# A gated, byte-quantized product and a signed layer on one Trainium2 core: bytes turned as 4-byte words, kv's bytes left in the low bytes of float16, and a list order chosen from 80 runs

## The chip, the cores and the metric

The kernel runs on one core of one Trainium2 chip. A core has a matrix engine (TensorE, "PE" in the profile; its weight loads are "PEld"), a vector engine (VectorE, "DVE"), a scalar engine (ScalarE, "ACT"), a general engine (GpSimd, "POOL") and a queue engine that issues the DMAs (SyncE, "SP"). Each works through its own list of instructions in order and waits on semaphores for the others. The metric is the time of one execution on the device in microseconds (us), smaller is better.

## The reference

`x` is float32 of 2 x 1024 x 2048, the context `kv` 2 x 2048 x 2048. What is computed, cut to the core:

```python
def fake_quant(x, scale, zp):
    q = jnp.clip(jnp.round(x / s + z), 0.0, 255.0)
    return (q - z) * s

def xattn(x1, x2):                       # scales and zero points are inputs, here 8/255 and 128
    return jnp.matmul(fake_quant(x1, ...), fake_quant(x2, ...))

def ffn(x, kernel, scale):               # kernel: 0/1, 2048 x 2048
    x_ei = jnp.concatenate([x[..., :1638], -4.0 * x[..., 1638:]], axis=-1)
    return scale * (x_ei @ kernel)

x = x + jnp.tanh(g_xattn[0]) * xattn(layernorm(x), ctx_4096)
x = x + jnp.tanh(g_ffn[0])   * ffn(layernorm(x), L0_ffn_kernel)
```

## The kernel before, in words

Rows of `x` come in 16 tiles of 128 rows: tiles 0 to 7 are the first batch, 8 to 15 the second. All large buffers are 4 KB-per-partition pages of one pool (44 of them).

**Product 1** (the quantized one). For each tile, VectorE takes the row statistics (`stats`, L362), small instructions make the row's factors, and `quant1` (L406 on ScalarE, L408 on VectorE) writes bytes `qn`. `shift1` (L414, ScalarE) subtracts 128, which makes bf16 or f16 values `q1`, and its accumulator gives the row sum `rsum`. The values are turned so that the contracted dimension lies on the partitions: tiles 0 to 3 by TensorE (`turn1`, L431, 16 transposes a tile into PSUM buffers `tr`, and `take1`, L423/L425, which copies them out), tiles 4 to 15 by a DMA transpose (`turn1_dma`, L441). `kv` is loaded in pieces of 128 x 1024 (`load_kv`, L445), quantized to bytes (`quant_kv`, L459 on ScalarE, L461 on VectorE) and shifted to bf16 or f16 (`shift_kv`, L468/L470) into pages `q2`. The matmuls of the first batch are `mm1` (L482): four column blocks of 512 by four pairs of tiles. Zero points other than 128 are put right with row sums (`tokb1`) and column sums: `sums_mm` (L494) lets TensorE add up a block's 16 slices with a matrix of ones, `sums_pair` (L503, L506) lets VectorE add them to two and leaves TensorE the last two (`sums_last`, L512). The results are added to `x` by `out1` (L524/L526), `add_row1` (L530) and `add_out1` (L534, GpSimd). In the second batch columns 0 and 1 go through one level of Strassen's scheme: seven products M1 to M7 per pair of tiles (`mm1s`, L584, `take1s` L596, `out1s` L603) over sums of halves made by VectorE (`right_sum` L547, `left_sum` L566/L568). Columns 2 and 3 are plain again.

**Product 2** (the layer with the 0/1 matrix). The normalized rows (`scale2` L623) are turned by TensorE as float32 (`turn2`, L630, `take2`), split into a high and a low float32r part (`part_hi` L676 on ScalarE, `part_lo` L680 on GpSimd or VectorE) and multiplied, again in Strassen's seven products, by slices of the matrix that ScalarE widens from bytes (`widen`, L720). The matmuls are `mm2` (L739): 1792 of 512 columns, the larger part of TensorE's work. `add2` (L754, VectorE) adds an accumulator to `back`, and `store2` stores it.

**The order.** Nothing above is issued as it is written. Each step is entered in a `Plan` with the engines that can do it and their costs (in units of some 0.22 us), the buffers that it reads, writes and opens, and, for the matmuls, a place in line. `Plan.dues` works out a due time for each step from the places of the matmuls that need it. `Plan.order` then walks once through time, gives each idle engine the ready step with the earliest due, and the resulting list is issued; that fixes every engine's instruction order. A step may begin once its due is nearer than `lead`; `port` marks VectorE steps that take turns with GpSimd in the plan. The pools' own semaphores keep the data right whatever the order.

```python
bytes_ = ctx.enter_context(tc.tile_pool(name="bytes", bufs=3))
BY_DMA = range(4, T)                      # tiles turned by a DMA
plan = Plan(dict(page=PAGES, acc=3, tr=2, q=3, qn=2, row=4, e=3, pair=2))
BY_PE = (True, True, True, False)         # blocks of the first batch summed by TensorE
order = plan.order({...}, {"SP": 13.0, "DVE": 22.0, "ACT": 22.0})
```

Of the kernel before, what the change touches and what calls it, by code (L numbers as in the profile page):

```python
# [19 lines left out]
P = 128  # L20
NB = 512
HB = 1024
EPS = 1e-5
CENTER = 128.0
# [3 lines left out]
class Op:  # L28
    __slots__ = ("engines", "f", "args", "deps", "users", "due", "lead", "opens", "uses",
                 "place", "end", "left", "index", "engine", "bias", "port")  # L30


class Plan:
# [21 lines left out]
    def op(self, engines, f, *args, reads=(), writes=(), opens=(), main=False, due=None, lead=80, bias=0.0,  # L55
# [7 lines left out]
        o.place = None  # L63
# [47 lines left out]
    def order(self, lag, start):  # L111


        self.dues()
        ready = {}
# [28 lines left out]
        while len(began) < len(self.ops):  # L144
            if not events:
                for e in engines:
                    if ready[e]:
                        print("stuck", e, [(o.f.__name__, o.args, o.due) for _, _, o in sorted(ready[e])[:4]])
                print(self.free, progress)
                raise RuntimeError("the plan is stuck")  # L150
# [5 lines left out]
            elif what == "idle":  # L156
                busy[o] = False
            else:
                for buf in o.uses:
                    if buf in self.count:  # L160
                        self.count[buf] -= 1
                        if not self.count[buf]:
                            self.free[self.kind[buf]] += 1
                for u in o.users:
                    u.left -= 1
                    u.end = max(u.end, now)
                    if not u.left:
                        for e in u.engines:
                            wait = 0.0 if e == o.engine and e != "SP" else lag.get((o.engine, e), lag[e])
                            push(now + wait, "ready", (e, u))  # L170
# [3 lines left out]
            while again:  # L174
                again = False
                for e in engines:
# [4 lines left out]
                    while ready[e]:  # L181
# [12 lines left out]
                        spare = 2 if o.due > progress + 40 else 0  # L194
# [24 lines left out]
        return [o for _, _, o in began]  # L219
# [3 lines left out]
def gated_xattn_ffn_kernel(  # L223
# [65 lines left out]
    kvv = kv.rearrange("b (k p) n -> b p k n", p=P)  # L289
# [17 lines left out]
    nc.vector.tensor_scalar(c2, z2, -1.0, CENTER, ALU.mult, ALU.add)  # L307
    f1 = const.tile([P, 1], F32, name="f1")
    nc.vector.tensor_scalar(f1, gate[:, 0:1], sc[:, 2:3], sc[:, 4:5], ALU.mult, ALU.mult)
    f1c1 = const.tile([P, 1], F32, name="f1c1")  # L310
# [4 lines left out]
    nc.vector.tensor_scalar(kc12, f1c1, c2, float(K), ALU.mult, ALU.mult)  # L315
# [5 lines left out]
    ident_bf = const.tile([P, P], BF, name="ident_bf")  # L321
    nc.vector.tensor_copy(ident_bf, ident)
# [6 lines left out]
    ones = const.tile([P, P], BF, name="ones")  # L329
    nc.gpsimd.memset(ones, 1.0)  # L330
# [3 lines left out]
    BY_DMA = range(4, T)  # L334
# [6 lines left out]
    DMA = 7.0  # L341
    ROOT = 8.0

    plan = Plan(dict(page=PAGES, acc=3, tr=2, q=3, qn=2, row=4, e=3, pair=2))
# [55 lines left out]
    def quant1(t: int, h: int, engine=None):  # L400

        if t not in qb:
            qb[t] = bytes_.tile([P, D], U8, tag="qn", name=f"qn_{t}", bufs=2)
# [6 lines left out]
    def shift1(t: int):  # L410

        q1[t] = page([D], F16 if t >= TPB else BF, f"q1_{t}")
        rsum[t] = small.tile([P, 1], F32, tag="rsum", name=f"rsum_{t}", bufs=8)
        nc.scalar.activation(q1[t], qb[t], AF.Copy, bias=-CENTER, accum_out=rsum[t])  # L414

    def tokb1(t: int):

        tokb[t] = small.tile([P, 1], F32, tag="tokb", name=f"tokb_{t}", bufs=T)
        nc.vector.tensor_scalar(tokb[t], rsum[t], f1c2, kc12, ALU.mult, ALU.add)
# [7 lines left out]
    def turn1(t: int, h: int):  # L427

        tr[t, h] = ps_tr.tile([P, KH, P], BF, tag="tr", name=f"tr1_{t}_{h}")
        for j in range(KH):  # L430
            nc.tensor.transpose(tr[t, h][:, j, :], q1[t][:, ts(h * KH + j, P)], ident_bf)  # L431

    def take1(t: int, h: int, engine=None):
        if h == 0:
            q1T[t] = page([KT, P], BF, f"q1T_{t}")
        copy(engine, q1T[t][:, ts(h, KH), :], tr.pop((t, h)))

    def turn1_dma(t: int):

        q1T[t] = page([KT, P], F16 if t >= TPB else BF, f"q1T_{t}")  # L440
        nc.sync.dma_start_transpose(out=q1T[t], in_=q1[t])  # L441

    def load_kv(b: int, c: int, g: int):
        stage[b, c, g] = page([2, NB], F32, f"kv_{b}_{c}_{g}")
        nc.sync.dma_start(stage[b, c, g], kvv[b, :, 2 * g : 2 * g + 2, ts(c, NB)])  # L445

    KEPT = ()

    def quant_kv(b: int, c: int, g: int, engine=None):

        if (b, c) in KEPT:
            if g % 4 == 0:
                qb[b, c] = page([4, HB], U8, f"q_{b}_{c}_{g // 4}")
            qb[b, c, g] = qb[b, c][:, g % 4, :]
        else:
            qb[b, c, g] = bytes_.tile([P, HB], U8, tag="q", name=f"q_{b}_{c}_{g}")
        v = flat(stage[b, c, g])
        if engine == "ACT":
            nc.scalar.activation(qb[b, c, g], v, AF.Identity, bias=z2, scale=rs2)  # L459
        else:  # L460
            nc.vector.tensor_scalar(qb[b, c, g], v, rs2, z2, ALU.mult, ALU.add)  # L461

    def shift_kv(b: int, c: int, g: int, engine=None):
        if g % 2 == 0:
            q2[b, c, g // 2] = page([4, NB], F16 if b else BF, f"q2_{b}_{c}_{g // 2}")
        half = flat(q2[b, c, g // 2][:, 2 * (g % 2) : 2 * (g % 2) + 2, :])
        if engine == "ACT":
            nc.scalar.activation(half, qb[b, c, g], AF.Copy, bias=-CENTER)  # L468
        else:
            nc.vector.tensor_scalar(half, qb[b, c, g], -CENTER, None, ALU.add)  # L470

# [18 lines left out]
    def sums_mm(b: int, c: int, ks):  # L490
        if ks[0] == 0:
            colsum[b, c] = ps_tr.tile([P, NB], F32, tag="tr", name=f"cs_{b}_{c}")
        for k in ks:
            nc.tensor.matmul(  # L494
                colsum[b, c], ones, rhs1(b, c, k), start=(k == 0), stop=(k == KT - 1)
# [18 lines left out]
    def row1(b: int, c: int):  # L514
        colrow[b, c] = rows.tile([P, NB], F32, tag="row", name=f"row_{b}_{c}")
        nc.scalar.activation(colrow[b, c], colsum.pop((b, c)), AF.Copy, scale=f1c1)

    def out1(b: int, c: int, tiles, i: int, engine=None):
# [4 lines left out]
        if engine == "ACT":  # L523
            nc.scalar.activation(ev[t, c], a, AF.Identity, bias=tokb[t], scale=f1)  # L524
        else:
            nc.vector.tensor_scalar(ev[t, c], a, f1, tokb[t], ALU.mult, ALU.add)  # L526
# [66 lines left out]
    def take1s(h: int, m: str, p: int):  # L593
        i, j = TAKES[m]
        xc = xt["x", 2 * p + i, h][:, ts(j, NB)]
        nc.vector.scalar_tensor_tensor(xc, acc1[SUM[m], h, p // 2][:, p % 2, :], f1, xc, ALU.mult, ALU.add)  # L596

    def out1s(h: int, m: str, p: int):
# [5 lines left out]
            ev[t, 2 * h + j], acc1[SUM[m], h, p // 2][:, p % 2, :], AF.Identity, bias=tokb[t], scale=f1  # L604
# [128 lines left out]

    def mm2(q: int, m: str, p: int, k: int, js=(0, 1)):
        if m in OPENS and k == 0:
            acc2[SUM[m], p] = ps_acc.tile([P, 2, NB], F32, tag="acc", name=f"acc2_{m}_{p}")
        for part in (hi, lo):
            for j in js:
                nc.tensor.matmul(  # L739
                    acc2[SUM[m], p][:, j, :],  # L740
# [11 lines left out]
    def add2(m: str, p: int, js=(0, 1)):  # L752
        v = back[(p,) + TAKES[m]][:, js[0] * NB : (js[-1] + 1) * NB]
        nc.vector.scalar_tensor_tensor(  # L754
            v, flat(acc2[SUM[m], p][:, js[0] : js[-1] + 1, :]), f2, v, ALU.mult, ALU.add
        )
# [15 lines left out]
    def ops_norm1(t: int, n: int, which: str, **when):  # L772
# [11 lines left out]
        for u in range(t, t + n):  # L784
            for h in range(2):
                op({"DVE": DVE(HB), "ACT": ACT(HB) + 0.9}, quant1, u, h, reads=[*both((which, u, h)), (("ra", u), 0)], writes=[(("qn", u), h)],
                   opens=[("qn", ("qn", u))] if h == 0 else [], port=True, **when)
            op({"ACT": ACT(D) + 0.9}, shift1, u, reads=both(("qn", u)), **when,
               writes=[(("q1", u), 0), (("rsum", u), 0)], opens=[("page", ("q1", u))])
            op({"DVE": 1.2}, tokb1, u, reads=[(("rsum", u), 0)], writes=[(("tokb", u), 0)], **when)  # L790
            if u in BY_DMA:
                op({"SP": 15.0}, turn1_dma, u, reads=[(("q1", u), 0)], writes=both(("q1T", u)),
                   opens=[("page", ("q1T", u))], **when)
                continue
            for h in range(2):
                op({"PE": 2.1}, turn1, u, h, reads=[(("q1", u), 0)], writes=[(("tr1", u, h), 0)],
                   opens=[("tr", ("tr1", u, h))], **when)
                op({"DVE": 3.2, "ACT": 4.6}, take1, u, h, reads=[(("tr1", u, h), 0)], writes=[(("q1T", u), h)],
                   opens=[("page", ("q1T", u))] if h == 0 else [], **when)

    def ops_kv(b: int, c: int, lead: float, by_pe: bool, lead2=None):

        lead2 = lead2 or lead
        for g in range(KG):
            v = (b, c, g)
            op({"SP": DMA}, load_kv, *v, writes=[(("kv",) + v, 0)], opens=[("page", ("kv",) + v)], lead=lead + 25)
            k = (("qb", b, c, g // 4), g % 4) if (b, c) in KEPT else (("qb",) + v, 0)
            op({"DVE": DVE(HB), "ACT": ACT(HB) + 0.9}, quant_kv, *v, reads=[(("kv",) + v, 0)], writes=[k],
               opens=[("page", k[0])] if (b, c) in KEPT and g % 4 == 0 else [] if (b, c) in KEPT else [("q", k[0])],
               lead=lead, port=True)  # L810
            w = ("q2", b, c, g // 2)
            op({"ACT": ACT(HB), "DVE": 3.3}, shift_kv, *v, reads=[k], writes=[(w, g % 2)],
               opens=[("page", w)] if g % 2 == 0 else [], lead=lead2, port=True)
# [68 lines left out]
    def ops_left_sums(p: int):  # L882
        for n, out, in0, in1 in ((3, "S3", "A11", "A21"), (1, "S1", "A21", "A22"), (2, "S2", "S1", "A11"),
                                 (4, "S4", "A12", "S2")):
            opens = [("page", ("q1S", p))] if n == 2 else []
            if n == 3:
                opens = [("page", ("q1S3", p))]
            op({"DVE": 3.3}, left_sum, p, n, reads=[half_key(p, in0), half_key(p, in1)],
               writes=[half_key(p, out)], opens=opens, lead=350.0, port=True)
# [10 lines left out]
    def ops_quad1(h: int, q: int):  # L900
# [11 lines left out]
        for m in ORDER1:  # L912
            acc = ("acc1", SUM[m], h, q)
            for p in pairs:
                for s in range(2):
                    op({"PE": 4.0}, mm1s, h, m, p, s, main=True, writes=[(acc, p % 2)],
                       reads=[half_key(p, LEFT1[m]), *both(right_key(m, h, s))],
                       opens=[("acc", acc)] if m in OPENS and p == pairs[0] and s == 0 else [],
                       in_turn=m in OPENS and p == pairs[0] and s == 0)
                i, j = TAKES[m]  # L920
                t = 2 * p + i
                v = ("x", t, h)
                if m in WITH_TOKENS:
                    e = ("e", t, 2 * h + j)
                    op({"ACT": 3.6}, out1s, h, m, p, reads=[(acc, p % 2), (("tokb", t), 0)], writes=[(e, 0)],
                       opens=[("e", e)], due=plan.place)
                    op({"POOL": GPS(NB)}, add_out1, 2 * h + j, t, reads=[(e, 0)], writes=[(v, j)], due=plan.place + 8)
                else:
                    op({"DVE": 3.6}, take1s, h, m, p, reads=[(acc, p % 2)], writes=[(v, j)], due=plan.place)
# [57 lines left out]
    def ops_product2(q: int, between):  # L987
        pairs = (2 * q, 2 * q + 1)
        for n, m in enumerate(ORDER):
# [25 lines left out]
            if q == T // 4 - 1 and n == len(ORDER) - 1:  # L1015
                steps[-LAG:] = tail
            for i, k, *js in steps:
# [3 lines left out]
                op({"PE": 2.1 * len(js)}, mm2, q, m, p, k, js, main=True, writes=[(acc, j) for j in js],  # L1021
                   reads=[(("hi", m, p), 0), (("lo", m, p), 0), (("wf", q, m, k), 0)],
                   opens=[("acc", acc)] if m in OPENS and k == 0 else [])
                if k == KH - 1:
                    v = ("back", p) + TAKES[m]
# [132 lines left out]
```

## Time and profile before

| | |
|---|---|
| median of 3 runs | 709.87 us (709.76 to 710.63) |
| the profiled execution, its own time | 710.47 us |
| its span, first to last instruction | 708.7 us |
| TensorE's clock | 1.000 of full, throughout |
| TensorE's first instruction, and its last record's end | 17.79 us, 704.46 us |
| ScalarE, VectorE, GpSimd busy | 482.6, 482.1, 306.5 us |
| DMA: moved, share of 16 engines | 162.07 MB, 68% |
| DMA packets under 512 B, of all | 29856 of 88396 |

How to read it: "busy" is the union of an engine's instruction records. Matmul records overlap (one lasts 0.38 us where one starts every 0.22 us), so TensorE's work is counted by the distance from one to the next. The span is what the instructions cover; the time of an execution is 1.8 us more in this one.

The last instructions, from the timeline (start us, length us, engine, line and operation, count, and in brackets the idle time before with what ended it):

```profile
702.00 0.75 DVE L754 SCALAR_TENSOR_TENSOR back<-acc_M,f,back 128x512 f32<-128x512 f32 x1 [1.89 <-PE acc_M L739]
...
702.81 0.50 PE L739 MATMUL acc_M<-wf_M,hi_M 128*128 128x512 f32 x1 [0.84 <-DVE back L754]
...
704.50 0.75 DVE L754 SCALAR_TENSOR_TENSOR back<-acc_M,f,back 128x512 f32<-128x512 f32 x1 [1.75 <-PE acc_M L739]
```

### The profile page before, as it was taken

The page shows a single profiled execution, that of the slowest core. Times are in us where ns is not written, and L with a number is a line of the kernel's source. Part 1 is how long each engine was busy: PE and PEld are TensorE (multiplying, and loading weights), DVE is VectorE, ACT ScalarE, POOL GpSimd, SP SyncE. Part 2 cuts the span into 40 slices and gives each one's busy share as a digit, 9 for nine tenths or more (in the row PEclk, how much of TensorE's full clock was granted, in tenths as well). Part 3 has the DMA queues.
Part 4 walks back from the last instruction along what each step waited for, and adds up shares of the span by engine and source line. Part 5 has one row for each costly group of instructions (what it writes and reads, how often), then busy time and mean ns, then how long its engine had stood idle before and what let it go on. Part 6 is the DMA issues. An engine that isn't in the chain of part 4 may idle for free.

```text
span 708.7 us, 8860 instructions
## 1 busy us (share of the span) xinstructions
PE 673.0 (95%) x3162; PEld 468.9 (66%) x3162; DVE 482.1 (68%) x725; ACT 482.6 (68%) x561; POOL 306.5 (43%) x186
## 2 busy tenths in 40 slices
PE   0699999999999999999999999999999999999997
PEld 0344444457778888878885444447888888888885
DVE  6989875799998778989978774458453335453331
ACT  4899853157689969989878832118689446679640
POOL 0048489983752403423337597874343001144000
PEclk9999999999999999999999999999999999999999
DMA  8999615959899999968589854338165279256032
GB/s 309 393 387 293 220 61 172 302 189 346 286 375 317 244 279 375 353 222 278 150 264 373 283 178 171 124 120 279 49 227 189 75 235 301 102 165 221 27 122 90
DMA packets 88396, 162.07 MB, mean 229 GB/s; under 512 B 29856, under 2 KB 46240, under 8 KB 88352
## 3 DMA queue, kind: packets, MB, share of 16 engines
q1 hardware_dynamic: 88352, 161.50, 68.4%
q8 instruction: 25, 0.41, 0.2%
q14 instruction: 19, 0.16, 0.1%
HBM read 117.44 MB, written 37.75 MB: 219 GB/s over the span
## 4 chain that ended last, share of the span: by engine, by line
PE 83%; DVE 6%; ACT 4%; POOL 3%; issue 2%; DMA 1%; SPq 0%; ACTq 0%; DVEq 0%; POOLq 0%
PE acc_M L739 53%; PE acc L482 19%; PE acc_M L584 6%; PE tr L630 3%; POOL x L534 2%; PE cs L494 2%; POOL x L530 2%; ACT wf_M L720 1%; DVE wB L705 1%; DMA x<-in_x_dram 1%; DVE bn_a L362 1%; DVE back L754 1%; DVE q L470 1%; ACT q L459 1%; ACT q L468 1%
## 5 line engine op out<-in xcount | busy, mean ns | idle before, releaser
L739 PE MATMUL acc_M<-wf_M,hi_M 128*128 128x512 f32 x896 | 282.2, 395 | 4.0 <-ACT wf_M L720 3.1
L739 PE MATMUL acc_M<-wf_M,lo_M 128*128 128x512 f32 x896 | 277.9, 391 | 0.5 <-POOL lo_M L680 0.5
L720 ACT ACTIVATE wf_M<-wr_M 128x1024 fp32r<-128x1024 uint8 x224 | 220.9, 1050 | 29.6 <-DMA wr_M<-in_wmask_dram 20.4
L739 PEld LDWEIGHTS acc_M<-wf_M,lo_M 128*128 128x128 f32 x896 | 168.1, 188 | 36.9 <-POOL lo_M L680 1.3
L739 PEld LDWEIGHTS acc_M<-wf_M,hi_M 128*128 128x128 f32 x896 | 163.9, 188 | 38.0 <-ACT wf_M L720 5.9
L482 PE MATMUL acc<-q,q1T 128*128 128x512 bf16 (+1 forms) x768 | 172.5, 382 | 0.5 <-DVE e L526 0.5
L680 POOL TENSOR_TENSOR lo_M<-A,hi_M 128x1024 fp32r<-128x1024 f32 x28 | 72.0, 2576 | 176.8 <-ACT hi_M L676 112.4
L754 DVE SCALAR_TENSOR_TENSOR back<-acc_M,f,back 128x1024 f32<-128x1024 f32 (+1 forms) x57 | 72.0, 1262 | 111.3 <-PE acc_M L739 96.3
L482 PEld LDWEIGHTS <-q1T 128*128 128x128 bf16 (+1 forms) x768 | 75.4, 98 | 90.5 <-issue 2.8
L530 POOL TENSOR_TENSOR x<-x,row 128x512 f32<-128x512 f32 x64 | 88.1, 1404 | 60.2 <-DMA kv<-in_kv_dram 38.0
L534 POOL TENSOR_TENSOR x<-x,e 128x512 f32<-128x512 f32 x64 | 91.9, 1454 | 42.7 <-ACT e L524 22.4
L524 ACT ACTIVATE e<-acc,tokb,f 128x512 f32<-128x512 f32 x30 | 22.7, 774 | 55.2 <-PE acc L482 50.7
L676 ACT CAST hi_M<-A 128x1024 fp32r<-128x1024 f32 x48 | 50.0, 1044 | 11.6 <-POOL A L664 7.9
L459 ACT ACTIVATE q<-kv,sc,rs 128x1024 uint8<-128x1024 f32 x41 | 49.8, 1232 | 5.3 <-DMA kv<-in_kv_dram 4.3
L362 DVE BATCH_NORM_STATS2 bn_b<-x 128x6 f32<-128x512 f32 x64 | 43.1, 686 | 14.9 <-POOL x L534 14.6
L423 ACT COPY A<-tr 128x512 f32<-128x512 f32 x33 | 19.2, 582 | 34.6 <-PE tr L630 34.6
L468 ACT ACTIVATE q<-q 128x1024 f16<-128x1024 uint8 (+1 forms) x39 | 40.3, 1046 | 0.4 <-DVE q L461 0.4
L526 DVE TENSOR_SCALAR e<-acc,f,tokb 128x512 f32<-128x512 f32 x18 | 14.5, 808 | 31.0 <-ACT e L524 26.9
L506 DVE TENSOR_TENSOR pair<-pair,q 128x1024 f16<-128x1024 f16 x30 | 30.8, 1033 | 2.9 <-ACT q L468 1.6
L414 ACT ACTIVATE q<-qn 128x2048 bf16<-128x2048 uint8 (+1 forms) x16 | 30.4, 1899 | 0.1
L680 DVE TENSOR_TENSOR lo_M<-A,hi_M 128x1024 fp32r<-128x1024 f32 x20 | 24.1, 1230 | 6.1 <-ACT hi_M L676 6.1
L461 DVE TENSOR_SCALAR q<-kv,rs,sc 128x1024 uint8<-128x1024 f32 x23 | 26.7, 1166 | 0.3
(99 smaller groups left out, 599.4 us busy)
## 6 DMA issues: line engine op xcount, KB each, us to landing
kv<-in_kv_dram SPq DMA_DIRECT2D x64, 512.0 KB, 9.9
x<-in_x_dram SPq DMA_DIRECT2D x32, 512.0 KB, 6.9
x<-x SPq DMA_DIRECT2D x32, 512.0 KB, 3.0
back<-x SPq DMA_DIRECT2D x32, 512.0 KB, 5.1
wr_M<-wt_T SPq DMA_DIRECT2D x32, 512.0 KB, 5.9
out_dram<-back SPq DMA_DIRECT2D x31, 512.0 KB, 4.1
wr_M<-in_wmask_dram SPq DMA_DIRECT2D x24, 512.0 KB, 5.9
n<-in_x_dram SPq DMA_DIRECT2D x16, 512.0 KB, 7.4
```

Of the source, the lines that this page charges most:

```text
L362: nc.vector.bn_stats(bn[v, t][:, c, :], xt[src[v, t, c // 2]][:, ts(c % 2, NB)])
L459: nc.scalar.activation(qb[b, c, g], v, AF.Identity, bias=z2, scale=rs2)
L468: nc.scalar.activation(half, qb[b, c, g], AF.Copy, bias=-CENTER)
L482: nc.tensor.matmul(acc1[b, c, tiles[0]][:, i, :], q1T[tiles[i]][:, k, :], rhs1(b, c, k), start=(k == 0), stop=(k == KT - 1),)
L530: nc.gpsimd.tensor_add(xc, xc, colrow[b, c])
L534: nc.gpsimd.tensor_add(xc, xc, ev.pop((t, c)))
L584: nc.tensor.matmul(acc1[key][:, i, :], left_half(p, LEFT1[m])[:, 4 * s + k, :], right1(m, h, s)[:, k, :], start=(m in OPENS and s == 0 and ...
L676: nc.scalar.copy(hi[m, p], A[left(m, p)])
L680: engines[engine].tensor_sub(lo[m, p], A[left(m, p)], hi[m, p].bitcast(F32))
L720: nc.scalar.activation(wf[q, m, k], wr[q, m, k // 4][:, k % 4, :], AF.Copy, bias=-float(RIGHT[m][1]))
L739: nc.tensor.matmul(acc2[SUM[m], p][:, j, :], part[m, p][:, k, :], wf[q, m, k][:, ts(j, NB)], start=(m in OPENS and k == 0 and part is hi), ...
L754: nc.vector.scalar_tensor_tensor(v, flat(acc2[SUM[m], p][:, js[0] : js[-1] + 1, :]), f2, v, ALU.mult, ALU.add)
```

## The change

1. **q1 is turned as bytes.** `shift1` and the DMA transposes go. `turn1` reads the 2048 bytes of a row as 512 float32 words: 4 transposes a tile, for all 16 tiles. `take1` reads the bytes of a word out of PSUM in steps of 4, subtracts 128 and writes f16. So slice 4w + j of the contracted dimension holds bytes j, j + 4, ...; `kv`'s rows are loaded in the same order ("(w p j)").
2. **Row sums** come from the bytes (`rowsum1`, ScalarE with its accumulator or VectorE's `tensor_reduce`), for tiles 0 and 1 from TensorE (`rowsum1_pe`, 16 matmuls of one column).
3. **kv's bytes stay bytes.** GpSimd fills a page with zeros (`fill_kv`), and `quant_kv` writes each byte into the low byte of a float16, which then is the byte times 2^-24. `shift_kv` goes. The factor 2^24 is put into the small constants (`f1u`, `f1c1u`), the zero point's 128 into others (`c2`, `kc12`, `kc12d`).
4. **Sums and orders.** Block 2 of the first batch goes from TensorE's sums to VectorE's pairs; the units of blocks and pairs run in another order; leads of the second batch change.
5. **Takes of the Strassen stage** are entered behind the matmuls of both pairs, and depend on the whole accumulator.
6. **The last pair's accumulator** for M5 and M3 is two single tiles of the pool `tr` instead of one of two halves.
7. **The list run** is repeated 80 times: each run shifts the due times of some steps, those that held up a matmul above all and others at random, and the list with the earliest planned end is issued.

```diff
-    def order(self, lag, start):
+    def order(self, lag, start, runs, seed=1):
...
+        for i in range(runs):
+            self.free, self.count = dict(free), dict(count)
+            try:
+                end = self.run(lag, start)
+            except RuntimeError:
+                end = None
+            if end is not None and (best is None or end <= best[0]):
+                best = end, self.began, [o.engine for _, _, o in self.began]
+                dues = [o.due for o in self.ops]
+                held = self.held_up()
+            for o, due in zip(self.ops, dues):
+                o.due = due
+            for ops in held:
+                if chance.random() < 0.5:
+                    step = chance.choice((3.0, 6.0, 12.0, 24.0))
+                    for o in ops:
+                        o.due -= step
...
-    kvv = kv.rearrange("b (k p) n -> b p k n", p=P)
+    kvv = kv.rearrange("b (w p j) n -> b p w j n", p=P, j=4)
...
+    def rowsum1_pe(t: int):
+        rsum[t] = ps_tr.tile([P, 1], F32, tag="tr", name=f"rs_{t}")
+        for k in range(KT):
+            nc.tensor.matmul(rsum[t], q1T[t][:, k, :], ones_h[:, 0:1], start=(k == 0), stop=(k == KT - 1))
...
-        for j in range(KH):
-            nc.tensor.transpose(tr[t, h][:, j, :], q1[t][:, ts(h * KH + j, P)], ident_bf)
+        for w in range(4):
+            nc.tensor.transpose(tr[t][:, w, :], qb[t].bitcast(F32)[:, ts(w, P)], ident)
...
+        v = flat(tr[t][:, 2 * h : 2 * h + 2, :]).bitcast(U8).rearrange("p (w t j) -> p w j t", w=2, j=4)
+        dst = q1T[t][:, ts(h, KH), :].rearrange("p (w j) t -> p w j t", j=4)
+        if engine == "ACT":
+            nc.scalar.activation(dst, v, AF.Copy, bias=-CENTER)
+        else:
+            nc.vector.tensor_scalar(dst, v, -CENTER, None, ALU.add)
...
+    def fill_kv(b: int, c: int, s: int):
+        q2[b, c, s] = page([4, NB], F16, f"q2_{b}_{c}_{s}")
+        nc.gpsimd.memset(flat(q2[b, c, s]).bitcast(F32), 0.0)
...
+        low = half.bitcast(U8).rearrange("p (n b) -> p n b", b=2)[:, :, 0]
...
+            nc.scalar.activation(low, v, AF.Identity, bias=z2, scale=rs2)
...
-    BY_PE = (True, True, True, False)
+    BY_PE = (True, True, False, False)
```

What this does to the lists of the engines, counted in the built programs: TensorE's transposes of q1 go from 64 of bf16 to 64 of float32 (4 a tile instead of 16, in 16 tiles instead of 4), sum matmuls from 48 and 10 to 32 and 12, and 32 one-column matmuls are new; L482 (768), L584 (224), L630 (256) and L739 (1792) keep their counts. ScalarE loses 39 shifts of kv and 16 of q1, and gets 22 half-tile takes instead of 4 and 7 row sums. VectorE loses 25 shifts, and gets 10 half-tile takes instead of 4, 7 row sums and 6 more halves of `part_lo`. GpSimd gets 32 fills and 6 halves of `part_lo` fewer.

## The prediction, made before the run

> **What bounds the kernel now.** The first view is the page: TensorE (PE) is busy 95% of the span, no other engine over 68%, and its idle slices are the first two and the last.
>
> ```profile
> span 708.7 us, 8860 instructions
> PE 673.0 (95%) x3162; PEld 468.9 (66%) x3162; DVE 482.1 (68%) x725; ACT 482.6 (68%) x561; POOL 306.5 (43%) x186
> ...
> PE   0699999999999999999999999999999999999997
> ```
>
> So two things can move the time: how early PE's steady stream starts, and how much issue time PE needs. The chain of waits, in order of time (start us, length, what), gives the start and the pitch of the matmuls:
>
> ```profile
> 1.19 5.44 DMA x<-in_x_dram
> ...
> 14.57 1.14 ACT qn L406
> 15.76 1.79 issue
> ...
> 20.85 1.22 ACT q L459
> 22.08 1.89 ACT q L414 x2
> 24.16 0.95 ACT q L468
> 25.21 1.01 PE cs L494 x2
> ...
> 170.73 0.44 PE tr L630 x4
> ...
> 447.23 31.94 PE acc L482 x148
> ...
> 516.99 70.88 PE acc_M L739 x312
> ```
>
> The chain runs load, statistics, quantize, ScalarE's pass from bytes to bf16 (L414, L468), and PE has work only from 25 us. The last two lines give pitches: a bf16 or f16 matmul 31.94/148 = 0.2158 us, a product-2 matmul 70.88/312 = 0.2272 us; L630 gives 0.11 us per float32 transpose. Durations of single records (272 ns for that transpose) overlap and are not added. Busy time by stretch (PE is the second figure) and PE's own waits:
>
> ```profile
> 0.00:17.70 17.70, 0.00 (x0) 0.00 (x0) 11.82 (x42) 8.64 (x11) 1.21 (x10) 1.00 0.88 309
> 17.70:45.00 27.30, 20.73 (x127) 11.02 (x128) 25.28 (x56) 24.49 (x28) 5.11 (x4) 1.00 1.04 390
> ...
> PE tr L431 <- ACT q L414: 17.8, 1, 17.8
> PE cs L494 <- ACT q L468: 5.5, 1, 5.5
> PE acc_M L739 <- ACT wf_M L720: 3.1, 3, 1.4
> PE acc_M L584 <- ACT e L603: 2.4, 3, 0.9
> PE acc_M L739 <- DVE back L754: 0.8, 1, 0.8
> ```
>
> By 45 us PE has issued 63 useful 512-column matmuls (127 less 64 transposes: 43 of L482, 20 of L494) and from there it is saturated. Check: after 45 us remain 1792 of L739 x 0.2272 = 407.1, 725 of L482 x 0.2158 = 156.5, 224 of L584 = 48.3, 256 transposes L630 x 0.11 = 28.2, 38 sum matmuls (28 of L494, 10 of L512) = 8.2: 648.3 us. From 45 us to PE's last record at 704.46 there are 659.5. PE thus loses 11.2 us after 45 us, of which the windows show 7.2 as idle; 4.2 us more follow PE (last add and store).
>
> **The change, part by part.**
>
> *Start.* Removed: the passes L414 (1.90 us a tile, plus 0.19 for the accumulator) and L468/L470 (1.05 or 0.69 us a half page) between quantizing and PE; now PE turns q1's bytes as float32 words, and kv is quantized straight into place. Loads land at 6.65 us and then one each 0.524 MB / 390 GB/s = 1.34 us. By the changed order (four x, nine kv, four x, kv again) load n lands at 6.65 + 1.34(n - 1): the eighth page of kv block 0 (n = 12) at 21.4, that of block 1 (n = 24) at 37.5. ScalarE quantizes tile 0 until 15.7 as before, PE turns it in 0.44, then two quantizations (2 x 1.23) stand before its two takes (1.1 each): the first matmul of the product at about 19.5 instead of 26. Tile 1's takes end near 23.5. Block 0 of the first pair, its sums and PE's row sums run until about 32, block 1 waits for its loads and ends at 37.5 + 0.8 (quantize) + 1.7 (eight matmuls) = 40.0. By then 64 of L482 and 32 sum matmuls are done: 96 against 63 at 45. The row sums (32 matmuls of one column, between 0.1 us, the weight load's row, and 0.22 each, so 3 to 7 us) lie in that wait for loads. If the loads came 2 us later, so would all.
>
> *Work on PE after that.* Product 2, L584 and L630 stay: 407.1 + 48.3 + 28.2. Of L482, 768 - 64 = 704 remain: 151.9. Sums: block 2 goes to VectorE pairs, so 12 matmuls: 2.6. New: 12 tiles turned by PE, 4 transposes each, 48 x 0.11 = 5.3 (the DMA transposes of 12 tiles go; 4 of the 16 tiles fall into the start). Total 643.4. [...]
>
> *Lost time.* Of the 11.2 us two parts should go: the last pair's accumulator becomes two tiles, so the 0.84 us for which PE waits on VectorE at 702 us goes; and product 1's takes move behind both pairs' matmuls, where PE is at the next accumulator, so up to 2.4 us on L603 go. New waits can come: each turned tile needs its bytes and one of two `tr` buffers in PE's order; behind a late one every matmul queues. Twelve such places at 0 to 0.4 us (the wait of L431 on DVE q1T, 0.4, is the nearest row): 0 to 4.8, I take 1. So 11.2 - 3.2 + 1 = 9.0; bounds 3 and 16.
>
> *Work put at nothing on the path.* ScalarE and VectorE lose 64 shifts (L468, L470; 64 us) and L414 (33 us). They gain 32 half-tile takes out of PSUM in 4-byte steps: VectorE 0.68 (L425) to 1.28 (L754), ScalarE 1.01 (L423) to 1.23: I take 1.1, 35 us. And 14 row sums: ScalarE 1.90 + 0.19; VectorE between 1.6 (twice L461's 0.80) and 2.7 (bn_stats' 1.33 ns an element): 2.2; 30 us in all. Quantizing now writes every second byte; no row shows that. Bounds: unchanged (0.81 and 1.23) and twice that; unchanged taken, since the input read is the same. POOL gains 32 fills of 128x1024: from 98 ns (128x1) and 204 ns (128x128) it is 0.95 each, 30 us; 16 fall into the first 20 us, where POOL sits idle until 39.9. In compensation six halves of `lo` (L680) go from POOL to VectorE, 1.23 each. Cover: from 45 to 155 us VectorE is busy 87 and ScalarE 67 of 110. In 282 to 375 us the cover is thin: 83 and 82 of 93.
>
> *Sum.* 40.0 + 643.4 + 9.0 + 4.2 = 696.6 us of span against 708.7. The profiled execution took 710.47, its span plus 1.8; the median shown, 709.87, is span plus 1.2. So 697.8 in the terms of the median, 1.7% less.
>
> **The rivals.**
>
> *The second batch gives part back.* In 282 to 375 us VectorE loses about 11 shifts (9.8) and gains some five row sums (11), six takes (6.6) and a few of the `lo` halves (3): 83 + 11 = 94 of 93 us. Also tiles 11 to 15 are now turned inside product 1's Strassen stage, whose takes, left sums and PE work follow one another closely. Speaks for it: a single POOL add holds a 0.8 us quantization for 2.9 us (L461's longest), and every fill is one more such holder. Against: in that order every take I followed by hand ends before PE arrives. Price 6 to 11 us: 704 to 709.
>
> *Slower: byte steps are dear.* If writes in 2-byte steps and reads in 4-byte steps take twice as long on both engines, the surplus is 1.0 us on each of 64 quantizations and 32 takes. The first batch absorbs its half (cover above) apart from 2.4 us at the start. In 282 to 375 us some 16 quantizations and 10 takes cost 26 us over two engines with 21 us of cover, less VectorE's 11: PE waits about 16. Total 697.8 + 2.4 + 16 = 716. It decides from about 0.8 us surplus each. [...]
>
> [...]
>
> *More gain.* If the repeated list run removes PE's lost time down to 3 us: 690.6 + 1.2 = 692 us.
>
> *It does not do what it says*: if tile 0's takes stand behind loads that land later than 18 us, ScalarE's order holds them as L468 does now, and the start gains only 1 to 2 us: about 701, within the forecast's range.
>
> **How the numbers follow.** Forecast (start at 39 to 44, lost time 4 to 14: 692 to 705) 0.72; part given back 0.12; slower 0.09; more gain 0.07. The range 691 to 706 takes in the forecast, the better rival and the lower third of the second batch's: about 0.82. A measurement here tells about 0.2% (1.4 us) from no change. Faster: 0.72 + 0.07 + nearly all of 0.12 = 0.88; same 0.03; slower 0.09.
>
> **What would show it.** First L482 equivalent near 19.5 us, steady PE from about 40; transposes of four in 0.44 us; quantize rows still 0.8 and 1.23; DMA free of transposes and PE's waits after 45 us at 4 to 6 us in sum. Wrong if quantize or take rows are near 2 us, or if waits of PE on takes or fills stand in the stretch 280 to 430 us.

## The result, and the profile after

| | before | after |
|---|---|---|
| median (lowest to highest of 4 runs) | 710.25 us (709.76 to 710.88) | 698.68 us (698.62 to 698.79) |
| ratio, 95% interval | | 0.9836 (0.9823 to 0.9848) |
| span of the profiled execution | 708.7 us | 697.0 us |
| last matmul record ends | 704.46 us | 692.57 us |
| DMA packets under 512 B | 29856 of 88396 | 4912 of 63580 |

The forecast was 697.8 us in a range of 691 to 706. Engine totals and the slices of the span, from the page after:

```profile
span 697.0 us, 8833 instructions
...
PE 674.0 (97%) x3180; PEld 471.7 (68%) x3180; DVE 490.2 (70%) x717; ACT 455.4 (65%) x536; POOL 316.8 (45%) x210
...
PE   1999999989999999999999999999999999999997
```

TensorE's busy time has hardly moved (673.0 before), so the 11.7 us came out of its idle time, 8.6 us of it before 45 us (TensorE is busy 29.29 us there, 20.73 before). ScalarE is busy 27 us less, VectorE 8 more, GpSimd 10 more. TensorE's waits after the change (us in total, times, longest):

```profile
PE cs L556 <- ACT q L530: 13.2, 1, 13.2
PE acc_M L809 <- ACT wf_M L782: 1.5, 2, 1.4
PE acc L544 <- DVE q1T L514: 0.8, 1, 0.8
PE acc_M L809 <- POOL lo_M L742: 0.6, 1, 0.6
...
PE acc_M L646 <- ACT e L665: 0.3, 1, 0.3
```

The first line is only the start: TensorE has work at 13.2 instead of 17.8 us. The waits on the last `add2` and, but for 0.3 us, on L665 (L603 before) are gone; no wait behind the start is longer than 1.4 us. TensorE's timeline at the start (start us, length us, instruction, count, idle before):

```profile
13.23 1.01 PE L556 MATMUL cs<-q,ones_h 128*128 128x512 f16 x2 [13.23 <-ACT q L530]
14.37 0.69 PE L503 MATMUL tr<-ident,qn 128*128 128x128 f32 x2
...
16.55 2.72 PE L556 MATMUL cs<-q,ones_h 128*128 128x512 f16 x6 [0.36 <-DVE r_a L447]
19.06 2.61 PE L544 MATMUL acc<-q,q1T 128*128 128x512 f16 x6
21.50 0.60 PE L503 MATMUL tr<-ident,qn 128*128 128x128 f32 x4
21.94 2.32 PE L544 MATMUL acc<-q,q1T 128*128 128x512 f16 x10
...
31.86 1.02 PE L544 MATMUL acc<-q,q1T 128*128 128x512 f16 x4
32.72 0.59 PE L556 MATMUL cs<-q,ones_h 128*128 128x512 f16 x2
33.16 1.03 PE L544 MATMUL acc<-q,q1T 128*128 128x512 f16 x4
```

The first matmul of the product starts at 19.06 (forecast 19.5). Until 21.5 us a matmul starts every 0.43 us ((2.72 - 0.58)/5, where 0.58 us is the length of one), from 21.94 on every 0.215 ((2.32 - 0.38)/9): the first matmuls run at half pace. In the last lines four product matmuls and two sum matmuls take 1.30 us (31.86 to 33.16), just as long as the issue of six matmuls, 6 x 0.2158: TensorE, not the load, sets the pace there. The row groups that the prediction priced (group | busy us, mean ns of one | idle before):

```profile
L522 POOL MEMSET q<- 128x1024 f32 x32 | 29.2, 952 | 5.1 <-DVE q L532 2.2 <-ACT q L530 1.6 <-PE acc_M L809 0.9
L512 ACT ACTIVATE q1T<-tr 128x1024 f16<-128x1024 uint8 x22 | 21.3, 1019 | 7.5 <-PE tr L503 6.8 <-POOL A L728 0.7
L480 DVE TENSOR_REDUCE rsum<-qn 128x1 f32<-128x2048 uint8 x7 | 15.8, 2273 | 0.0
L514 DVE TENSOR_SCALAR q1T<-tr 128x1024 f16<-128x1024 uint8 x10 | 11.9, 1211 | 0.1
L530 ACT ACTIVATE q<-kv,sc,rs 128x1024 uint8<-128x1024 f32 x45 | 53.5, 1236 | 7.8 <-DMA kv<-in_kv_dram 5.1 <-POOL q L522 2.5
```

A byte written into every second place costs ScalarE 1236 ns, as before (1.23 us); on VectorE the median is 811 ns (0.81 before). The takes in steps of four bytes are 1.02 and 1.21 us.

The last two `add2` run at 690.79 and 692.60 us, and no matmul waits for the first of them:

```profile
690.79 0.75 DVE L825 SCALAR_TENSOR_TENSOR back<-acc_M,f,back 128x512 f32<-128x512 f32 x1 [1.44 <-PE acc_M L809]
692.60 0.75 DVE L825 SCALAR_TENSOR_TENSOR back<-acc_M,f,back 128x512 f32<-128x512 f32 x1 [1.06 <-PE acc_M L809]
```

### The profile page after: what moved, and what is told of

It is laid out like the page before. It is cut to its first block, busy times and chain, and to the rows that moved or that the text cites. A ratio compares the mean times of both kernels' runs of the same rounds, so it can differ in the third digit from the quotient of the medians.

```text
span 697.0 us, 8833 instructions
## 1 busy us (share of the span) xinstructions
PE 674.0 (97%) x3180; PEld 471.7 (68%) x3180; DVE 490.2 (70%) x717; ACT 455.4 (65%) x536; POOL 316.8 (45%) x210
## 2 busy tenths in 40 slices
DMA packets 63580, 155.78 MB, mean 223 GB/s; under 512 B 4912, under 2 KB 21296, under 8 KB 63536
## 4 chain that ended last, share of the span: by engine, by line
PE 87%; DMA 4%; DVE 4%; POOL 2%; ACT 2%; issue 1%; SPq 0%; ACTq 0%; DVEq 0%
PE acc_M L809 57%; PE acc L544 19%; PE acc_M L646 7%; PE tr L692 4%; DMA kv<-in_kv_dram 3%; DMA x<-in_x_dram 1%; POOL x L596 1%; DVE wB L767 1%; ACT wf_M L782 1%; POOL x L592 1%; PE tr L503 1%; DVE qn L472 0%; PE cs L574 0%; DVE x L685 0%; DVE bn_b L426 0%
## 5 line engine op out<-in xcount | busy, mean ns | idle before, releaser
L544 PE MATMUL acc<-q,q1T 128*128 128x512 f16 x768 | 171.6, 381 | 1.2 <-DVE q1T L514 0.8
L742 POOL TENSOR_TENSOR lo_M<-A,hi_M 128x1024 fp32r<-128x1024 f32 x24 | 62.1, 2586 | 179.5 <-ACT hi_M L738 160.1
L544 PEld LDWEIGHTS <-q1T 128*128 128x128 f16 x768 | 75.2, 98 | 90.2 <-issue 1.9
L592 POOL TENSOR_TENSOR x<-x,row 128x512 f32<-128x512 f32 x64 | 88.6, 1408 | 43.8 <-ACT sd_a L438 15.5
L530 ACT ACTIVATE q<-kv,sc,rs 128x1024 uint8<-128x1024 f32 x45 | 53.5, 1236 | 7.8 <-DMA kv<-in_kv_dram 5.1
L586 ACT ACTIVATE e<-acc,tokb,f1u 128x512 f32<-128x512 f32 x34 | 25.1, 774 | 49.6 <-PE acc L544 47.8
L742 DVE TENSOR_TENSOR lo_M<-A,hi_M 128x1024 fp32r<-128x1024 f32 x24 | 33.7, 1421 | 7.2 <-ACT hi_M L738 7.2
L568 DVE TENSOR_TENSOR pair<-pair,q 128x1024 f16<-128x1024 f16 x36 | 36.6, 1022 | 2.5 <-ACT q L530 0.8
L728 POOL TENSOR_TENSOR A<-A,A 128x1024 f32<-128x1024 f32 x8 | 21.1, 2648 | 23.7 <-DVE A L726 16.4
L522 POOL MEMSET q<- 128x1024 f32 x32 | 29.2, 952 | 5.1 <-DVE q L532 2.2
L512 ACT ACTIVATE q1T<-tr 128x1024 f16<-128x1024 uint8 x22 | 21.3, 1019 | 7.5 <-PE tr L503 6.8
L767 DVE SCALAR_TENSOR_TENSOR wB<-wB,wB 128x2048 uint16<-128x2048 uint16 x8 | 24.2, 3031 | 0.0
```

What stands on the lines that cost most here:

```text
L530: nc.scalar.activation(low, v, AF.Identity, bias=z2, scale=rs2)
L544: nc.tensor.matmul(acc1[b, c, tiles[0]][:, i, :], q1T[tiles[i]][:, k, :], rhs1(b, c, k), start=(k == 0), stop=(k == KT - 1),)
L568: nc.vector.tensor_add(colsum[b, c], colsum[b, c], v[:, i : i + 2, :])
L592: nc.gpsimd.tensor_add(xc, xc, colrow[b, c])
L742: engines[engine].tensor_sub(lo[m, p], A[left(m, p)], hi[m, p].bitcast(F32))
```

## The experiments

Theory A is that of the prediction: the gain is the start, and there the passes that went. Its rivals are that one part alone gives it: q1's way, kv's way, the order of the units, or the repeated list run. "Slower" and "faster" are against the changed kernel, 698.68 us, if not said otherwise; all were measured beside the kernel before, which gave 710.1 to 710.6 us in every set.

**1. The list run once** (`..., 80, 2)` becomes `1, 2)`).

> The changed kernel with the list run once instead of 80 times; everything else stays. Theory A (the gain is the passes and transposes that left the way from the load to the first matmul, and the order of the loads): 697 to 701 us, PE's first product matmul still near 19 us and steady by 42. Rival B (the repeated list run makes the gain): 704 us or more, with PE's waits after 45 us back at the 7 us of the kernel before.

Measured 699.97 us (699.87 to 700.05), ratio 0.9848 (0.9834 to 0.9863): 1.3 us of 11.6. The wait on L665 is back at 1.2 us. So nearly all of the gain is there without the search.

**2. The search alone** (the kernel before, its list run repeated 80 times with the same seed).

> The kernel before with nothing but the list run repeated 80 times (the same search and seed as in the changed kernel). Theory A: 706 to 711 us, since PE starts as late as before and loses at most 11 us after 45 us. Rival B (the search is a large part): 703 or less.

Measured 719.29 us (718.88 to 719.34), 1.0127 (1.0112 to 1.0142): 9.0 us slower than before and above both ranges, although the planned end of its list was earlier (3249.2 units against 3259.2). TensorE waits longer (2.4 us on L603 before, here L659: 5.4) and in places where it hadn't:

```profile
PE cs L550 <- DVE q L526: 15.0, 1, 15.0
PE tr L686 <- DVE A L700: 5.8, 1, 5.8
PE acc_M L640 <- ACT e L659: 5.4, 6, 0.9
PE tr L487 <- DVE q1T L481: 4.0, 3, 2.2
```

The planner's costs don't know the chip's waits: an end that is 2 us earlier in the plan was 9 later on the chip.

**3. Another seed, more runs** (`300, 4`, planned end 3253.8 units against 3268.4 of the changed kernel, 3.2 us earlier).

> The changed kernel with 300 list runs from another seed, whose planned end is 14.6 units (3.2 us) earlier than the list of the changed kernel. If the plan's end tells the chip's: 695 to 696.5 us. If it does not (what PE loses is down to 7 us, and the plan's model of loads is not that fine): 697.5 to 701.

Measured 705.36 us (704.69 to 706.37), 0.9929 (0.9912 to 0.9946): 6.7 us slower than the list that was issued, and above both ranges. The order of a list for the same work has thus moved the time by 1.3, 6.7 and 9.0 us in these three experiments (by 4.4 and 9.1 us between the two lists of experiments 5 and 6 below), and two kernels with different lists can't be compared to better than that. This concerns 5 to 8 below, and is why two of them were repeated with the list run once.

**4. 64 more transposes** (each tile turned twice into the same place).

```diff
-        for w in range(4):
+        for w in (0, 1, 2, 3, 0, 1, 2, 3):
```

> Each turned tile is turned twice into the same buffer: 64 more float32 transposes, same list. By the pitch of 0.11 us: 12 or 13 tiles in the steady stream cost 0.44 each, 5.3 to 5.7 us, and the start little: 704 to 705. [...]

Measured 703.69 us (703.62 to 703.98): 5.0 us more. 52 of the doubled transposes lie behind 41.4 us, where TensorE has little slack: 0.096 us each, or 0.11 with the 0.6 us by which the wait on L514 became shorter (0.8 to 0.2 us). The prediction's 0.11 us from one to the next holds, and the length of one record (273 ns, median, here) is no price.

**5. q1's way back** (second pass to float16, 64 float16 transposes for four tiles, DMA transposes for twelve; kv's way and the order stay).

> q1 by the old way within the changed kernel: ScalarE's pass of 1.90 us to float16 with its accumulator, tiles 0 to 3 turned by TensorE in 16 transposes, tiles 4 to 15 by DMA, row sums from the accumulator; kv's side stays, with its rows in plain order. Theory A: the first product matmul comes 2 x 1.9 us or more later (near 23 to 25 us), PE saves 12 x 0.44 us of transposes later: 698 to 703 us in sum. Rival C (q1's way is the whole gain): 706 us or more.

Measured 705.03 us (703.97 to 705.80), between the two ranges, but for another reason than the turning: the float16 identity matrix that these transposes need was cast by VectorE. In the start's timeline of that kernel (VectorE's and GpSimd's instruction):

```profile
5.16 10.88 DVE L386 CAST ident_h<-ident 128x128 f16<-128x128 f32 x1
```

```profile
2.58 13.38 POOL L514 MEMSET q<- 128x1024 f32 x15
```

A cast of 128x128 took 10.88 us: it ended when the row of 15 fills of zeros ended. All statistics queued behind it, and TensorE began at 18.0 us. In the next kernel GpSimd makes that matrix itself, ahead of the fills.

> As e8_q1_old, but the float16 identity is made by GpSimd ahead of its fills: in e8 VectorE's cast of it stood 10.9 us behind the fills and held the first statistics back until 16 us. Theory A (both byte parts count, kv's more): 699 to 703 us, first product matmul near 23 us. Rival C (q1's way, not the accident, made e8's 705): 704 to 706.

Measured 697.85 us (696.64 to 698.51), 0.9824 (0.981 to 0.9839): 0.8 us faster than the whole change, below theory A's range; the intervals of the ratios overlap. Its first product matmul starts at 22.86 us, 3.8 later, and TensorE then has 48 transposes less to do (5.3 us). The same with the list run once:

> q1's way alone put back (second pass to float16, 64 float16 transposes for four tiles, DMA transposes for twelve, identity made by GpSimd ahead of the fills), the list run once, against 699.97 us of the changed kernel with one list run. Theory (the 4-byte turn gives 3.8 us at the start and takes 5.3 us of TensorE later, with waits in its favour or against it of some 1 us): 697 to 700 us. Rival (the 4-byte turn saves waits on the DMA transposes and on ScalarE, and the search hid that): 703 us or more.

Measured 702.25 us (700.99 to 702.75), 2.3 us slower than experiment 1 and between the two ranges. With the search -0.8, without it +2.3: turning q1 as 4-byte words is worth nothing that stands out from the luck of a list. What it gives at the start it takes as transposes later.

**6. kv's way back** (byte buffer, second pass to float16 with no fills; q1's way and the order stay, but q1's bytes have two buffers instead of three, to make room).

```diff
+        qb[b, c, g] = bytes_.tile([P, HB], U8, tag="q", name=f"q_{b}_{c}_{g}")
...
+            nc.scalar.activation(qb[b, c, g], v, AF.Identity, bias=z2, scale=rs2)
...
+    def shift_kv(b: int, c: int, g: int, engine=None):
...
+        copy(engine, half, qb[b, c, g])
```

> kv by the old way within the changed kernel: quantized to a byte buffer, then a second pass widens it to float16 (64 passes of 1.05 us on ScalarE or 0.69 on VectorE are back, the 32 fills go; three byte buffers for kv and two instead of three for q1, for space). q1's side stays. Theory A: the first block's pages come one pass later and the stretch 282 to 375 us is as full as before: 2 to 5 us slower than the changed kernel, 701 to 704. Rival C (kv's passes were hidden; only q1's way counts): 698 to 700.

Measured 709.36 us (708.63 to 710.52), 0.9985 (0.9975 to 0.9994): 10.7 us slower than the whole change, above theory A's range. With the list run once:

> kv's way alone put back as before (byte buffer, second pass, no fills), the list run once, so it stands against the changed kernel with one list run (699.97 us) without the search's luck. Theory (a quarter to a half of the gain is kv's shorter way: 64 passes less on ScalarE and VectorE and a first product matmul that does not wait for one): 704 to 709 us, PE's first product matmul 0.5 to 1 us later, and new waits of PE on ScalarE and VectorE after 45 us of 3 to 7 us in sum. Rival (the passes lay beside PE's work and cost only their place at the start): 700 to 702 us. Rival 2 (the searched list was what cost 709.36 us in the first try): below 700.

Measured 718.49 us (717.79 to 720.01), 1.0118 (1.0103 to 1.0133): 18.5 us slower than experiment 1, more than any theory expected. The windows of that kernel, then of experiment 1 (stretch, its length; busy of PE, PEld, DVE, ACT, POOL; clock, DMA share, GB/s):

```profile
282.00:375.00 93.00, 91.20 (x422) 74.22 (x421) 84.20 (x70) 72.47 (x79) 41.83 (x16) 1.00 0.60 201
375.00:435.00 60.00, 55.08 (x264) 27.40 (x263) 51.17 (x60) 53.25 (x57) 40.77 (x28) 1.00 0.76 272
```

```profile
282.00:375.00 93.00, 92.95 (x426) 73.50 (x425) 68.72 (x64) 69.44 (x75) 45.70 (x27) 1.00 0.65 223
375.00:435.00 60.00, 58.84 (x281) 27.70 (x280) 50.89 (x59) 42.32 (x48) 50.95 (x38) 1.00 0.75 268
```

VectorE gets 15.5 us of work back in the first stretch and ScalarE 11 in the second, and TensorE idles 1.8 and 4.9 us there (0.05 and 1.2 in experiment 1). Over the whole span the two engines are busy 30.7 and 35.8 us more (508.0 and 491.5 against 477.3 and 455.7), about the 64 us of passes that the prediction had counted. Between 45 and 627 us TensorE idles 10.5 us more in all, by 45 us it has issued 91 useful matmuls instead of 101 (2.2 us), and up to 3.4 us come from the clock, which the last section shows. Of the 18.7 us of span, 2.6 or more are not traced. Three of TensorE's waits in that kernel:

```profile
PE tr L692 <- DVE A L497: 3.7, 2, 2.6
...
PE acc L544 <- ACT q1T L512: 2.4, 2, 1.3
PE acc L544 <- ACT q L495: 2.2, 2, 1.8
```

Only the third, and 0.5 us more of that kind, is a wait on the second pass itself, all before 45 us; the others are on copies and takes that the busier engines finish late. The missing third buffer of q1 has a share that isn't known: ScalarE waits for such a buffer for 1.0 us in this kernel and 1.5 us in the one with the search (on L480), and nothing was run with that alone.

**7. The old order of the units** ((0, 0), (0, 1), (1, 0), ...: block 0 for two pairs before block 1).

> Units of the first batch in the old order: both first pairs of tiles in block 0 before block 1 of the first pair. The loads follow: x of tiles 2 and 3 is needed earlier. Theory A (at the start PE is bound by the loads and its own work together): the second pair's tiles are late, PE waits 1 to 4 us between 30 and 45 us: 699 to 702. Rival D (the order of units makes no difference, the list sorts it out): 698 to 699.

Measured 704.10 us (703.67 to 704.87), 0.9908 (0.9893 to 0.9923): 5.4 us slower and above both ranges. At 45 us TensorE has issued 74 product matmuls and 18 sum matmuls, 92 against 102, which is 2.2 us. Up to 3.4 us are two falls of the clock (last section), one of them at 150 us, far from the start. So 5.4 us is not the price of the order of the units alone, and it is less than a list by itself can make.

**8. Block 1's sums given to VectorE as well** (`BY_PE = (True, False, False, False)`, seed 3). This asks whether TensorE's own work holds the start.

> Block 1's column sums given to VectorE's pairs as well (16 sum matmuls become 2), list chosen from 80 runs with another seed. Theory (TensorE's issue is the bound from about 31 us on, in the start too): 14 matmuls of 0.2158 us = 3.0 us less, 695 to 697 us, block 1 of the first pair paced by the loads alone (1.34 us a page). Rival (VectorE is late with the pair sums, 16 of 0.69 to 1.4 us more at the start): sums late, TensorE waits on DVE, 700 us or more.

Measured 705.75 us (705.38 to 706.53), 0.9937 (0.9923 to 0.9952). The first half of the expectation is there: the 64 product matmuls of the first pair are issued by 40.7 us, 41.1 with the four transposes that are still to come, where the changed kernel needs until 42.7 for both; on the way TensorE waits for quantized pages (0.28, 0.74 and 1.10 us on L530). Then all of it is lost: 1.36 us on a late L470 and 2.71 us on ScalarE's take L512, and later 2.4 us on L742 and 1.7 us on L706. The late sums on VectorE that the rival expected aren't there.

**9. The last pair's accumulator as one buffer again**, same list.

> Only the last pair's accumulator put back as one buffer of two halves, with the same list. Theory (the edit took out the 0.84 us that TensorE waited for VectorE's last add): 699.4 to 699.6 us, and PE waits about 0.8 us on DVE back again just before its last matmuls. Rival (the wait was hidden, since the last matmul and add follow at once anyway): 698.7 us, no wait.

Measured 699.84 us (699.82 to 700.02): 1.2 us slower, 0.2 above the theory's range, and TensorE's waits have the line again:

```profile
PE acc_M L810 <- DVE back L826: 0.8, 1, 0.8
```

So the split accumulator is worth what its wait cost, and 0.3 us on top.

## Why the prediction was right

Its sum, by its own terms:

| term | predicted | measured |
|---|---|---|
| steady stream reached | 40.0 us | 42.7 us |
| TensorE's work after that | 643.4 | 643.4 (the same counts at the same prices) |
| lost time | 9.0 | 6.5 |
| end after TensorE's last record | 4.2 | 4.4 |
| span | 696.6 | 697.0 |

The second column works so: at 41.4 us TensorE had issued 60 product matmuls, 32 sum matmuls and 12 transposes; the four and four that were to be done by then are 4 x 0.2158 + 4 x 0.11 = 1.3 us more. TensorE's work isn't measured by itself, so the lost time is what is left between 42.7 + 643.4 and the last record at 692.57. Two terms were off by 2.5 us or more, one each way, and cancel: that the sum comes within 0.4 us is luck.

*Start.* The first product matmul and the order of the loads came as forecast; by 45 us 102 useful matmuls are out against 63. The step that was mis-sized is "block 1 waits for its loads and ends at 40.0". TensorE isn't waiting for loads there: its first matmuls go at half pace (twelve between 16.55 and 21.5 us, where twelve at 0.2158 take 2.6, so 2.4 us lost), and from 21.9 to 41.4 us it has gaps of 0.28 and 0.38 us only. The kernel before had shown the half pace too (eight L482 in 3.62 us from 26.02 us, in 1.89 us later on), and the sum has no term for it. Nor are the loads the last to come: block 1's last page, which was forecast to land at 37.5 and to be quantized in 0.8 us, is quantized from 40.15 to 40.95 us, behind bytes of q1 (L472) on VectorE. The gap for the row sums doesn't exist, and they need none: 16 one-column matmuls take 0.41 us to the start of the next one, 32 of them 0.8, not 3 to 7. With 16 sum matmuls less before that point (experiment 8) it came at 41.1, so loads and quantizing alone would have been some 1.1 us behind the forecast, TensorE's pace the other 1.6; that split rests on another list.

*Work after that.* The pitches hold (a product-2 matmul 0.227 us at the end of the trace), and the transposes cost 0.10 us by experiment 4. At the length of a record, 273 ns, experiment 4's 52 transposes would have cost an estimated 14.2 us (52 x 0.273); 5.0 were measured.

*Lost time.* Both parts that were to go went (0.84 and 2.4 to 0.3 us), the first confirmed by experiment 9. The 1 us for late transposes is the 0.8 on L514. Product 2's waits on `widen` fell from 3.1 to 1.5 us, which hadn't been forecast; with experiment 1's list they are 1.6, with experiment 3's 3.9. Behind 45 us the windows show 2.8 us of idle, where the prediction looked for waits of 4 to 6.

*Work put at nothing.* Every new row came near its price: takes 1.02 and 1.21 (1.1), row sums 1.92 on ScalarE (1.90) and 2.27 on VectorE (2.2), fills 0.95, quantizing unchanged (1.24 on ScalarE, 0.81 on VectorE). So the rival "byte steps are dear" had its mechanism refuted by L530 and L532 alone.

*"The second batch gives part back"* fell too. It had VectorE at 94 of 93 us in 282 to 375; it was busy 70.8 (83.0 before). Three row sums and two takes fell to VectorE in that stretch, 9.2 us instead of the 17.6 assumed; the list gave ScalarE 22 of the 32 takes. VectorE's nine passes (8.4 us) went, near the 9.8 assumed. The rest is the order of the list: of the combining of product 2's operands (L660 to L666, 9.0 us there before) 1.2 us is left in that stretch, and quantizing takes 10.4 us instead of 15.2.

*Where the gain comes from.* In the account of the table, counted from 45 us for the kernel before as the prediction does, the 11.7 us of span are 2.3 us of earlier stream (45.0 to 42.7), 4.9 us less work behind it (648.3 to 643.4) and 4.7 us less lost time (11.2 to 6.5), less 0.2 at the end. By the parts undone: kv's shorter way 10.7 us (18.5 with one list run), the order of the units 5.4, the list run 1.3, the split accumulator 1.2, q1's way nothing. These don't add up to 11.6, since each kernel also has a list of its own; only the split accumulator was tried on the list as it stands. A list alone has moved the time by up to 9 us, so of the parts only kv's way stands out, and there q1's third buffer went as well. That the change as a whole is faster is more than the luck of a list, as far as lists were tried: three of the changed kernel gave 698.7, 700.0 and 705.4 us, two of the kernel before 710.3 and 719.3. Its size is not: with experiment 3's list the forecast of 697.8 us would have been 7.6 us too low, and 705.4 near the upper end of its range. That the order of the list is worth so much by itself wasn't in the prediction, except for 6 us of "more gain"; it could as well have hidden half of the gain. Which part of kv's way counts, ScalarE's and VectorE's freed time or the shorter chain from load to matmul, is not told apart beyond the waits and the idle time in the two stretches.

## What to carry to other kernels

Price a change on TensorE by the distance between starts (here 0.096 us a transpose whose record lasts 0.273), and start that account only where its matmuls have reached full pace (here 0.215 us a matmul from 21.9 us on, 0.43 before). Work taken off engines that are busy 68% mattered here to the engine that is busy 95%: with kv's 64 passes put back, TensorE idled 10.5 us more in many short waits. A schedule that is chosen by a plan's own end has to be measured, since the plan may well choose a slower one; and an edit that changes the schedule has to be compared on several of them.

## What was not expected

**A wait can cost more than its length.** In several of these kernels the granted clock falls in the middle of the run. Experiment 8's timeline shows the wait (start, length, instruction, idle before), its windows of 1 us the clock (column behind POOL's):

```profile
45.65 1.01 PE L574 MATMUL cs<-pair,ones_h 128*128 128x512 f16 x2 [2.71 <-ACT q1T L512]
```

```profile
45.00:46.00 1.00, 0.35 (x1) 0.10 (x1) 1.00 (x2) 1.00 (x2) 0.00 (x0) 0.58 1.05 387
46.00:47.00 1.00, 1.00 (x4) 0.41 (x3) 1.00 (x2) 1.00 (x1) 0.00 (x0) 0.50 1.07 391
47.00:48.00 1.00, 1.00 (x4) 0.32 (x3) 1.00 (x2) 1.00 (x4) 0.00 (x0) 0.50 1.06 389
48.00:49.00 1.00, 1.00 (x4) 0.34 (x3) 1.00 (x3) 1.00 (x2) 0.86 (x1) 0.71 1.05 387
49.00:50.00 1.00, 1.00 (x6) 0.49 (x5) 1.00 (x3) 1.00 (x3) 1.00 (x2) 1.00 1.02 377
```

For 3.4 us the clock is half, and a matmul starts every 0.43 us instead of every 0.215 (the number behind x counts the records that lie in a window, overlapping ones too): the missing shares of the clock, 0.42 + 0.50 + 0.50 + 0.29, are 1.7 us, of which 0.2 fall into the wait itself and the rest is lost on top of its 2.7. The same came with a wait of 2.79 us in experiment 3 (at 157 us), one of 2.40 in experiment 7 (at 150), one of 2.58 in the kernel with kv's way back and the list run once (at 160), and 5.8 us in experiment 2, where the clock was low for 6.8 us. Two shorter waits close together did it too (1.6 and 1.3 us, at 50 us in the kernel with kv's way back and the list run once; 1.9 and 0.7, at 23 us in experiment 7). The changed kernel, whose longest wait behind the start is 1.4 us, and the kernel before show 1.00 from the first matmul to the last. By the loss of clock alone, experiment 7's 5.2 us of span hold up to 3.4, experiment 3's 7.6 up to 1.7. So part of what a bad list costs is this.

The length of the wait alone doesn't decide. Experiment 8 has another one, and behind it the clock stays at 1.00:

```profile
151.79 0.73 PE L809 MATMUL acc_M<-wf_M,lo_M 128*128 128x512 f32 x2 [2.39 <-POOL lo_M L742]
```

The traces show where the difference lies. Within one execution the falls lie whole numbers of 3.413 us apart, the last fall, behind the last matmul, included: in experiment 8 at 45.17 and 703.94 us (193.0 such steps), in experiment 7 at 23.46, 149.75 and 702.71 (37.0 and 162.0), in experiment 3 at 157.53 and 703.66 (160.0). Cut the execution into such steps, counted back from its last fall. Each of the seven falls before the end follows a step in which TensorE was idle for 2.20 us or more of the 3.41, in one wait or two; behind 30 us no step with less is followed by one, and the largest of these has 1.94 us (in the kernel with q1's way back and the list run once). Experiment 8's second wait is divided by the edge at 150.98 us, 1.58 us before it and 0.82 behind. So of two waits of the same length, 2.40 us in experiment 7 and 2.39 in experiment 8, the one with 2.20 us in one step was followed by a fall and the one with no more than 1.58 us in one step was not. Where the steps lie differs between executions (the first edge 0.90 us behind the first instruction of the changed kernel's, 2.98 in experiment 7's).

The half pace at the very start, 0.43 us a matmul until 21.5 us, is of the same size, though the profile's clock column says 1.00 there. It ends on such an edge: counted back from the changed kernel's last fall at 697.22 us, one lies at 21.38.

**A VectorE copy lasted until a row of fills on GpSimd ended**: 10.88 us for a 128x128 cast (experiment 5), which began while the fills ran and ended within 0.1 us of their end; in the kernel before, with GpSimd idle, a cast of that size took 0.22 us. In the changed kernel one quantization by VectorE that began beside the same fills (14.23 us; they end at 15.95) took 2.27 us instead of 0.81, while the statistics at the start ran on beside them (VectorE busy 12.3 of the first 17.7 us, 11.8 before).
